# An adaLN block with a Mamba2 scan: the norm's application behind a decayed product, the gates' rows spread over three engines, the signs one step later

## The chip, the cores and the metric

The kernel runs on one core of a Trainium2 chip. The metric is the device time of one execution in microseconds (us), as the median of several runs. The core's engines work in parallel, each through its own instructions in a fixed order: TensorE (PE, matrix products and transposes, its weight loads shown as PEld), VectorE (DVE), ScalarE (ACT), GpSimd (POOL) and SyncE (SP), which here issues most of the DMA transfers.

## The reference

The input x has 4 sequences of 512 tokens with 512 features. A row `c` for each sequence gives six modulation vectors, two of which are gates.

```python
x = L0_attn_input_
mod = (_silu(L0_c) @ L0_wmod).reshape(L0_c.shape[0], 6, 1, -1)
sa, ca, ga, sb, cb, gb = (mod[:, 0], mod[:, 1], mod[:, 2], mod[:, 3], mod[:, 4], mod[:, 5])
ga = (2 * (ga >= 0) - 1) * jnp.maximum(jnp.abs(ga), 0.25)
gb = (2 * (gb >= 0) - 1) * jnp.maximum(jnp.abs(gb), 0.25)
h = _layernorm(x, axis=-1) * (1 + ca) + sa
x = x + ga * _L0_attn_ref(h, ...)
h = _layernorm(x, axis=-1) * (1 + cb) + sb
x = x + gb * _L0_ffn_ref(h, L0_ffn_weight, L0_ffn_bias)
```

`_L0_attn_ref` is a Mamba2 block. One projection gives x, B, C, z and the step dt. x, B and C go through a causal convolution over 4 tokens and a SiLU. A scan in chunks of 128 tokens follows with 64 heads of 16 features; B and C have 64 states in 8 groups. Within a chunk, token s contributes to token l with the weight C·B times exp(-(sum of dt between them)): this is the "decay". The result, times SiLU(z), is projected back to 512 features. `_L0_ffn_ref` is one 512x512 layer whose weights are replaced by their signs, times the mean magnitude of each row (alpha), plus a bias.

## The kernel before

**Tiling and steps.** A sequence is cut into two halves of 256 tokens, eight halves h in all; a half has two chunks c, and a chunk four pairs gp of head groups. A pair is a unit (h,c,gp): 64 units, one for each step of the loop at L845. In one step the kernel first emits what its list `steps` holds for that step, then the C·B products of two new units (`burst`, every other step), then `stage2` of the step's unit (its products with the decay, py) and last `stage0` and `stage1` of the unit two steps ahead, the "newest" one.

**The decays.** There are four decay tiles of 128x1024, two (r=0 and r=1) for a unit, so a tile is used by every second unit. `stage0` has SP load the sums into it by two DMAs (`load_sums`, L541 and L542, 256 and 128 KB); they can go when PE has read the tile for the last time. `stage1` makes the mask `gm`, has ACT take eight exps for each tile (L549) and DVE multiply by the mask (L625, "the decayed product"). `stage2` then has PE take py from it. Some decays of the last half are made ahead in the space of the projection's weights (`AHEAD`).

**The next half's front.** `FRONT` (L787) says at which step, counted from eight steps ahead of the half, each part is emitted: the load of x, then `f_norm` (the first layer norm) at step 2, `f_hT` at step 3 (PE's transposes phT, L330, and ACT's application of the modulation into hT, L347), `f_dt` (pa, L368), the projections pp_B, pp_C, pp_x (L434) with their convolutions on DVE (u_B, u_C, u_x, L454), and pp_z with uz (L516).

**The tails.** After a chunk's four units, `tail1` (L729) projects the result back (po), multiplies by the gate, adds the residual (xr) and takes the second layer norm into t. `tail2` comes a step later (PE's transposes ph at L757, ACT's h at L759), `tail3` two steps later (pf, L775; o at L777 and L778; the store res<-o by SP at L779).

**The layer norm.** `layer_norm` (L289) takes statistics on DVE, a power on POOL (rs, L298), and applies them on DVE at L300, at once. The tile t is single (`bufs=1`).

**The gates' rows.** `late_mods` (L233, once, in the second step) makes four of the modulation rows as one tile of 128x512, four lanes of which hold each vector, at lanes 0, 32, 64 and 96. Its last part (L250 to L262) makes the two gates and gate times bias on DVE and stores them by SP to `gate_d`; `load_gates` (L717) later spreads them over all lanes for a sequence, 768 KB. SP takes its DMAs in order: one that waits for its data holds up those behind it. Behind these stores stands, among others, the load of `wout` (L265).

**The signs.** `signs(o)` (L269) loads 128 rows of the ffn weights, sums their magnitudes on DVE (L274), takes the signs on DVE (L277) and scales them on ACT (L278). It runs for o=0 to 3 at steps 2 and 3, and `turned_signs` transposes them from step 5 on.

**Order.** A scheduling layer keeps the order of emission for each engine, apart from what is placed by `tc.issue_after(...)`: that makes the instructions inside it come after the one named, on their engines' lists. The fences `newest[...]` hold the last instruction of a kind for that use.

Of the kernel before, what the change touches and what calls it, by code (L numbers as in the profile page):

```python
# [11 lines left out]
F32 = mybir.dt.float32  # L12
AF = mybir.ActivationFunctionType
ALU = mybir.AluOpType
AX = mybir.AxisListType
# [3 lines left out]
B, L, DM = 4, 512, 512  # L19
# [8 lines left out]
NHALF = B * L // T  # L28
# [12 lines left out]
def adaln_mamba_block(  # L41
# [15 lines left out]
    nc = tc.nc  # L57
# [6 lines left out]
    def bc_mid(ap, n):  # L64

        return ap.unsqueeze(1).to_broadcast([ap.shape[0], n, ap.shape[1]])
# [4 lines left out]
    wk = ctx.enter_context(tc.tile_pool(name="wk", bufs=2))  # L71
# [47 lines left out]
    gate_d = dram.tile([B, 3, DM], F32, name="gate_d")  # L119
# [25 lines left out]
    def load_wm_at(t6, place, k0=0):  # L145

        n = place.shape[1]
        nc.sync.dma_start(place, wm_v[:, k0 : k0 + n, t6 * DM : (t6 + 1) * DM])
        for k in range(n):
            wms[t6, k0 + k] = place[:, k]  # L150
# [27 lines left out]
    room = wk.tile([P, 3, DM], F32, tag="gates", name="wm3_g", bufs=1)  # L178
    room_z = wm_tiles(3, "z", 6, 2)

    def load_late(h):

        load_wm_at(2, wout[:, 0:NK])
        load_wm_at(5, wout[:, NK:])
        load_wm_at(4, bwT)
        for k in range(2):
            load_wm_at(3, room_z[k].unsqueeze(1), k)
        load_wm_at(3, room[:, 0:2, :], 2)


    sc = keep.tile([P, NK, 32], F32, name="sc")
# [17 lines left out]
    def glued(products, after=None):  # L209

        with tc.issue_after(after) if after else nullcontext():
            first = products[0]()  # L212
        with tc.issue_after(first.ins), tc.high_priority(offset=1000):
            for product in products[1:]:
                product()  # L215
# [17 lines left out]
    def late_mods(h):  # L233

        pg = ps.tile([P, DM], F32, tag="mm", name="pg")
        glued([
            partial(
                mm, pg[32 * j : 32 * j + 32, :], sc[:, k, :], wms[t6, k], start=(k == 0), stop=(k == NK - 1)
            )
            for k in range(NK) for j, t6 in enumerate((2, 5, 4, 3))  # L240
        ])
        row = wk.tile([P, DM], F32, tag="t", name="rows", bufs=1)
        nc.vector.tensor_copy(row, pg)
        pm = ps.tile([P, NK, P], F32, tag="mm", name="pm")
        for dt in range(NK):
            nc.tensor.transpose(pm[:, dt, :], row[:, dt * P : (dt + 1) * P], ident)
        nc.vector.tensor_copy(modT[:, 2], pm[:, :, 96 : 96 + B])
        nc.vector.tensor_scalar(modT[:, 3], pm[:, :, 64 : 64 + B], 1.0, None, ALU.add)

        g = row[0:64, :]  # L250
        sg = wk.tile([64, DM], F32, tag="h2", name="sg")
        ab = wk.tile([64, DM], F32, tag="h2", name="ab")
        brow = wk.tile([64, DM], F32, tag="th", name="brow")
        second = slice(32, 32 + B)
        nc.sync.dma_start(brow[second, :], ffn_b.partition_broadcast(B))
        nc.vector.tensor_scalar(sg, g, 0.0, 2.0, ALU.is_ge, ALU.mult)
        nc.vector.scalar_tensor_tensor(ab, g, -1.0, g, ALU.mult, ALU.max)
        nc.vector.tensor_scalar(ab, ab, 0.25, None, ALU.max)
        nc.vector.scalar_tensor_tensor(sg, sg, -1.0, ab, ALU.add, ALU.mult)
        nc.vector.tensor_mul(ab[second, :], sg[second, :], brow[second, :])  # L260
        for i, v in enumerate((sg[0:B, :], sg[second, :], ab[second, :])):
            nc.sync.dma_start(gate_d[:, i, :], v)  # L262

    def load_wout():
        nc.sync.dma_start(wout, w_outT.rearrange("(k p) e -> p k e", p=P))  # L265
# [3 lines left out]
    def signs(o):  # L269

        fw = wk.tile([P, DM], F32, tag="h2", name=f"fw{o}")
        nc.sync.dma_start(fw, ffn_w[o * P : (o + 1) * P, :])
        alpha = wk.tile([P, 1], F32, tag="rs1", name=f"alpha{o}")
        nc.vector.tensor_reduce(alpha, fw, AX.X, ALU.add, apply_absolute_value=True)  # L274
        sw = wk.tile([P, DM], F32, tag="CB"[o % 2], name=f"sw{o}", bufs=3)

        nc.vector.tensor_scalar(sw, fw, 0.0, 0.5, ALU.is_ge, ALU.subtract)  # L277
        nc.scalar.activation(sw, sw, AF.Identity, scale=alpha)  # L278
        sws[o] = sw
# [9 lines left out]
    def layer_norm(tiles, name, into=None):  # L289
        n = len(tiles)  # L290
        st = wk.tile([P, n, 6], F32, tag=f"st{n}", name=f"st_{name}")
        mv = wk.tile([P, n, 2], F32, tag=f"mv{n}", name=f"mv_{name}")
        rs = wk.tile([P, n], F32, tag=f"rs{n}", name=f"rs_{name}")
        for j, t in enumerate(tiles):
            nc.vector.bn_stats(st[:, j, :], t)
            nc.vector.bn_aggr(mv[:, j, :], st[:, j, :])
        nc.vector.tensor_scalar(rs, mv[:, :, 1], EPS, None, ALU.add)
        nc.gpsimd.tensor_tensor(rs, rs, mhalf[:, :n], ALU.pow)  # L298
        for j, t in enumerate(tiles):
            nc.vector.tensor_scalar(  # L300
                into[j], t, mv[:, j, 0:1], rs[:, j : j + 1], ALU.subtract, ALU.mult
            )


    H = [dict(B={}, C={}, xt={}, xs={}, bt={}, z={}) for _ in range(NHALF)]
# [132 lines left out]
    newest = {}  # L438
# [105 lines left out]
    def exps(h, c, gp, ets):  # L544
        hd0 = c * NH + gp * HPP
        for r in range(2):
            for i in range(HPG):
                hd = hd0 + r * HPG + i
                nc.scalar.activation(  # L549
                    ets[r][:, i, :], ets[r][:, i, :], AF.Exp, bias=H[h]["st"][:, hd : hd + 1], scale=-1.0  # L550
                )
# [60 lines left out]
    def stage1(h, c, gp):  # L612

        n = f"{h}_{c}_{gp}"
        ets, e = U0.pop((h, c, gp))
        gm = wk.tile([P, 2, CH], F32, tag="gm", name=f"gm_{n}", bufs=3)  # L620
        nc.vector.tensor_mul(gm, G.pop(((h, c, gp), 0)), bc_mid(upto, 2))
        if (h, c, gp) not in AHEAD:
            exps(h, c, gp, ets)
        for r in range(2):
            nc.vector.scalar_tensor_tensor(  # L625
                ets[r], ets[r], 1.0, bc_mid(gm[:, r, :], HPG), ALU.min, ALU.mult
            )
        U1[h, c, gp] = (ets, e)

    def stage2(h, c, gp):  # L630
# [84 lines left out]
    gates = {}  # L715
# [13 lines left out]
    def tail1(h, c):  # L729
        b = h // HPB  # L730
        x2 = tails[h, c]
        po = ps.tile([P, DM], F32, tag="mm", name=f"po_{h}_{c}")
        last = (h, c) == (NHALF - 1, 1)
        for g in range(NKI):
            if last and g == NKI - 2:

                with tc.issue_after(last_po.ins):
                    tail2(h, 0)
            last_po = mm(po, H[h]["z"][g // 2][:, g % 2, c * CH : (c + 1) * CH], wout[:, g, :],  # L739
                         start=(g == 0), stop=(g == NKI - 1))  # L740
        t = wk.tile([P, DM], F32, tag="t", name=f"t_{h}_{c}", bufs=1)
        nc.vector.tensor_mul(t, po, gates[b][:, 0, :])
        nc.vector.tensor_add(x2, x2, t)
        layer_norm([x2], f"f{h}_{c}", [t])
        nc.gpsimd.tensor_add(x2, x2, gates[b][:, 2, :])
        tails[h, c] = (x2, t)
        if last:
            with tc.issue_after(last_po.ins):
                tail3(h, 0)
# [64 lines left out]
    def at(step, f, *args):  # L814
        steps.setdefault(step, []).append((f, args))

    for h in range(NHALF):
        for step, f, args in (FIRST, SECOND)[h] if h < 2 else FRONT:
            at(max(0, h - 1) * NU + step, f, h, *args)
        if h % HPB == 0:  # L820
            at(h * NU + 3, load_gates, h // HPB)
        if h == 0:
            at(0, load_late, h)
            at(1, behind, 0, late_mods)
            at(2, load_wout)
            for o in range(NK):
                at(o // 2 + 2, signs, o)
    for o in range(NK):
        at(o // 2 + 5, behind, 1, turned_signs, o)
    for h in range(NHALF):  # L830
# [9 lines left out]
    h = NHALF - 1  # L840
# [4 lines left out]
    for step in range(-1, max(steps) + 1):  # L845
        for f, args in steps.get(step, []):
            f(*args)

        new = units[step + 2 : step + 3] if step >= 0 else units[0:2]
        if step < 0:  # L850
            burst([], new)
            for unit in new:
                stage0(*unit)
                stage1(*unit)
        elif step < len(units):
            if step % 2 == 0 and (step + 2 < len(units) or not is_first(*units[step][:2])):
                burst(units[step : step + 2], units[step + 2 : step + 4])
            stage2(*units[step])
            for unit in POST.get(step, []):
                ahead(*unit)  # L860
            for unit in new:
                stage0(*unit)
                stage1(*unit)


_OUT = ((B, L, DM), np.float32)
# [39 lines left out]
```

## Time and profile before

| | |
|---|---|
| median of 3 runs | 736.62 us (733.73 to 736.94) |
| profiled execution | 737.38 us, of which the span from first to last instruction is 735.7 |
| mean granted TensorE clock | 0.993 |
| PE busy | 700.4 us (95%) |
| DVE, ACT, POOL busy | 599.5 (81%), 522.0 (71%), 254.8 us (35%) |
| HBM traffic | 92.47 MB read, 5.79 MB written |
| L549, decay exps on ACT | 960 instructions, 293.9 us |
| L625, decayed products on DVE | 120 instructions, 160.8 us |

The page gives busy times of the engines, and a chain of work that ended last, with its share by engine. The timeline gives for each instruction or run of like ones its start, its duration, engine, line, operation and tiles, and in brackets how long the engine was idle before it and what released it. Windows give the busy time of each engine in a stretch, with the granted clock of TensorE and the moved bytes.

### The profile page before, as it was taken

Reading aid. Unit: us, or ns where it says so; the run is one execution under the profiler, and the core shown is the slowest. Engines: PE = TensorE matmul, PEld = TensorE weight load, DVE = VectorE, ACT = ScalarE, POOL = GpSimd, SP = SyncE. Lnnn points to the kernel's source line nnn. Section 1 sums busy time; section 2 is a strip of 40 time slices with the busy share of each in tenths; the row PEclk is TensorE's granted clock in tenths of the full one; section 3 lists DMA queues with packets and bytes.
Section 4 is the critical chain, followed back from the end, with each engine's and each line's share of the span. In section 5 each row is a group of like instructions: output and inputs, shape, how many; then the busy total and the mean of one; then the engine's idle time right before and its main releaser. Section 6 shows DMA issues by size and latency. Waiting matters only on the chain.

```text
span 735.7 us, 15007 instructions
## 1 busy us (share of the span) xinstructions
PE 700.4 (95%) x5196; PEld 500.8 (68%) x5196; DVE 599.5 (81%) x1170; ACT 522.0 (71%) x1507; POOL 254.8 (35%) x297
## 2 busy tenths in 40 slices
PE   6999979899999999999999999999999999999997
PEld 3786746666677666677677666776667866677754
DVE  3869888876998678986899768996799867996995
ACT  2467658748696697785976787865968768788941
POOL 4021323444243332343223342433414332333652
PEclk9999989999999999999999999999999999999999
DMA  8991693535555256444644256552564537457720
GB/s 279 328 291 41 204 208 85 135 98 142 127 132 144 63 155 137 102 115 102 159 116 130 53 116 168 142 137 53 140 132 114 130 86 176 116 150 151 142 69 29
DMA packets 119067, 99.24 MB, mean 135 GB/s; under 512 B 73984, under 2 KB 97152, under 8 KB 118992
## 3 DMA queue, kind: packets, MB, share of 16 engines
q1 hardware_dynamic: 117808, 96.39, 52.3%
q0 software_dynamic: 896, 1.38, 0.7%
q8 instruction: 41, 0.67, 0.4%
q10 hardware_dynamic: 288, 0.52, 0.2%
q14 instruction: 34, 0.28, 0.1%
HBM read 92.47 MB, written 5.79 MB: 134 GB/s over the span
## 4 chain that ended last, share of the span: by engine, by line
PE 65%; ACT 16%; DVE 9%; DMA 4%; issue 4%; POOL 1%; SPq 1%; ACTq 0%; DVEq 0%; POOLq 0%
PE po L739 14%; PE pp_x L434 11%; PE pp_z L434 10%; ACT decay L549 9%; PE pp_C L434 7%; PE pp_B L434 5%; PE pf L775 3%; PE py L212 2%; PE py L215 2%; DVE decay L625 2%; ACT h L759 2%; DVE u_x L454 2%; DMA fw<-in_ffn_w 2%; ACT win L549 2%; PE gy L215 2%
## 5 line engine op out<-in xcount | busy, mean ns | idle before, releaser
L549 ACT ACTIVATE decay<-decay,st 128x128 f32<-128x128 f32 x960 | 293.9, 395 | 4.2 <-DMA decay<-sums_d 3.7
L625 DVE SCALAR_TENSOR_TENSOR decay<-decay,gm 128x1024 f32<-128x1024 f32 x120 | 160.8, 1341 | 50.3 <-ACT decay L549 47.2
L434 PE MATMUL pp_x<-hT,win 128*128 128x259 f32 x512 | 120.7, 390 | 7.3 <-DVE u_C L454 7.3
L434 PE MATMUL pp_z<-hT,win 128*128 128x256 f32 x512 | 118.1, 383 | 0.0
L434 PEld LDWEIGHTS pp_x<-hT,win 128*128 128x128 f32 x512 | 96.9, 193 | 25.2 <-ACT decay L549 7.7
L739 PE MATMUL po<-wout,z 128*128 128x512 f32 x256 | 113.8, 595 | 0.0
L434 PEld LDWEIGHTS pp_z<-hT,win 128*128 128x128 f32 x512 | 94.3, 189 | 16.3 <-issue 3.5
L675 POOL TENSOR_TENSOR z<-yt,z 128x256 f32<-128x256 f32 x62 | 62.9, 1015 | 76.1 <-DVE yt L674 57.8
L454 DVE SCALAR_TENSOR_TENSOR u_x<-pp_x,cw,u_x 128x256 f32<-128x256 f32 x192 | 83.6, 474 | 1.3 <-ACT u_x L450 0.7
L739 PEld LDWEIGHTS po<-wout,z 128*128 128x128 f32 x256 | 47.5, 190 | 53.1 <-issue 52.4
L672 POOL TENSOR_TENSOR yt<-yt,xs 128x256 f32<-128x256 f32 x46 | 41.4, 899 | 106.3 <-DVE yt L671 78.6
L507 POOL TENSOR_TENSOR xs<-u_x,rr 128x512 f32<-128x512 f32 x32 | 42.7, 1334 | 79.2 <-DVE u_x L459 61.3
L516 ACT ACTIVATE uz<-pp_z,zb 128x256 f32<-128x256 f32 x64 | 27.5, 470 | 59.0 <-PE pp_z L434 59.0
L215 PE MATMUL py<-decay,xpad 128*32 128x128 f32 x1680 | 66.3, 276 | 0.0
L434 PE MATMUL pp_B<-hT,win 128*128 128x259 f32 x256 | 63.5, 396 | 2.7 <-ACT decay L549 1.9
L434 PE MATMUL pp_C<-hT,win 128*128 128x259 f32 x256 | 59.6, 384 | 1.1 <-DVE u_x L454 1.1
L775 PE MATMUL pf<-bwT,h 128*128 128x512 f32 (+1 forms) x136 | 59.0, 578 | 1.4 <-ACT h L759 1.3
L434 PEld LDWEIGHTS pp_B<-hT,win 128*128 128x128 f32 x256 | 47.4, 193 | 14.5 <-ACT decay L549 3.1
L450 ACT ACTIVATE u_x<-pp_x,cb,cw 128x256 f32<-128x256 f32 x64 | 35.3, 560 | 30.5 <-PE pp_x L434 30.4
L434 PEld LDWEIGHTS pp_C<-hT,win 128*128 128x128 f32 x256 | 47.8, 189 | 9.4 <-PE pn L424 1.4
L679 POOL TENSOR_TENSOR xd<-xpad,st 128x256 f32<-128x256 f32 x48 | 34.1, 727 | 55.8 <-PE pst L215 28.3
L212 PE MATMUL py<-decay,xpad 128*32 128x128 f32 x240 | 47.4, 279 | 3.2 <-issue 2.2
(157 smaller groups left out, 1080.9 us busy)
## 6 DMA issues: line engine op xcount, KB each, us to landing
decay<-sums_d SPq DMA_DIRECT2D x120, 256.0 KB
decay<-sums_d SPq DMA_DIRECT2D x120, 128.0 KB
rr<-r_d SPq DMA_DIRECT2D x64, 128.0 KB
e<-e_d SPq DMA_DIRECT2D x96, 64.0 KB
win<-in_w_inT SPq DMA_DIRECT2D x4, 1024.0 KB
xr<-in_x SPq DMA_DIRECT2D x16, 256.0 KB
res<-o SPq DMA_DIRECT2D x15, 256.0 KB
x<-in_x SPq DMA_DIRECT2D x14, 256.0 KB
```

The costliest lines, as they stand in the source:

```text
L212: first = products[0]()
L215: product()
L434: last = mm(pm, win[:, k, col : col + P], H[h]["hT"][:, k, lo:], start=(k == 0), stop=(k == NK - 1))
L450: nc.scalar.activation(u[:, j, :], pm[:, KS - 1 :], AF.Identity, bias=cb[:, t : t + 1], scale=cw[:, t, KS - 1 : KS])
L454: nc.vector.scalar_tensor_tensor(u[:, j, :], pm[:, k : k + T], cw[:, t, k : k + 1], u[:, j, :], ALU.mult, ALU.add)
L507: nc.gpsimd.tensor_tensor(xs, xc, rr, ALU.mult)
L549: nc.scalar.activation(ets[r][:, i, :], ets[r][:, i, :], AF.Exp, bias=H[h]["st"][:, hd : hd + 1], scale=-1.0)
L625: nc.vector.scalar_tensor_tensor(ets[r], ets[r], 1.0, bc_mid(gm[:, r, :], HPG), ALU.min, ALU.mult)
L672: ew.tensor_add(t, t, xs)
L675: ew.tensor_mul(zg, t, zg)
L739: last_po = mm(po, H[h]["z"][g // 2][:, g % 2, c * CH : (c + 1) * CH], wout[:, g, :], start=(g == 0), stop=(g == NKI - 1))
L775: mm(pf, h2[:, k, :], bwT[:, k, cols], start=(k == 0), stop=(k == NK - 1))
```

## The change

Three edits.

1. `layer_norm` no longer applies its statistics at once. The application goes as a function into a list `normed`, and at the end of the step, after `stage1` of the newest unit, everything in the list is issued behind `newest["decay"]`, the r=0 decayed product of that unit. Excepted are the first half's first norm and the last half's two tails (`AT_ONCE`). The add of gate times bias to xr goes into the list too, when there is one.
2. The gates' rows are made at step 2 in a function of their own, `late_gates`: one operation on DVE, the magnitude on ACT, three operations on POOL, and the stores go by POOL's queue. Their tiles lie in `room`, the place of the gates' tile, not in the slots of h2 and th; the bias is loaded with the late weights.
3. `signs` come one step later, and the sum of magnitudes is taken by ACT as it writes the magnitudes (`accum_out`), not by DVE.

```diff
@@ load_late
         load_wm_at(3, room[:, 0:2, :], 2)
+        nc.sync.dma_start(brow[second, :], ffn_b.partition_broadcast(B))
@@ late_mods
-        g = row[0:64, :]
-        sg = wk.tile([64, DM], F32, tag="h2", name="sg")
-        ab = wk.tile([64, DM], F32, tag="h2", name="ab")
-        brow = wk.tile([64, DM], F32, tag="th", name="brow")
-        second = slice(32, 32 + B)
-        nc.sync.dma_start(brow[second, :], ffn_b.partition_broadcast(B))
-        nc.vector.tensor_scalar(sg, g, 0.0, 2.0, ALU.is_ge, ALU.mult)
-        nc.vector.scalar_tensor_tensor(ab, g, -1.0, g, ALU.mult, ALU.max)
-        nc.vector.tensor_scalar(ab, ab, 0.25, None, ALU.max)
-        nc.vector.scalar_tensor_tensor(sg, sg, -1.0, ab, ALU.add, ALU.mult)
-        nc.vector.tensor_mul(ab[second, :], sg[second, :], brow[second, :])
+        late_row.append(row)
+
+    late_row = []
+    second = slice(32, 32 + B)
+    brow = room[0:64, 2, :]
+
+    def late_gates(h):
+        g = late_row.pop()[0:64, :]
+        sg, ab = room[0:64, 0, :], room[0:64, 1, :]
+        nc.vector.tensor_scalar(sg, g, 0.0, 0.5, ALU.is_ge, ALU.subtract)
+        nc.scalar.activation(ab, g, AF.Abs)
+        nc.gpsimd.tensor_scalar(ab, ab, 0.25, 2.0, ALU.max, ALU.mult)
+        nc.gpsimd.tensor_tensor(sg, sg, ab, ALU.mult)
+        nc.gpsimd.tensor_tensor(ab[second, :], sg[second, :], brow[second, :], ALU.mult)
         for i, v in enumerate((sg[0:B, :], sg[second, :], ab[second, :])):
-            nc.sync.dma_start(gate_d[:, i, :], v)
+            nc.gpsimd.dma_start(gate_d[:, i, :], v)
@@ signs
-        nc.vector.tensor_reduce(alpha, fw, AX.X, ALU.add, apply_absolute_value=True)
         sw = wk.tile([P, DM], F32, tag="CB"[o % 2], name=f"sw{o}", bufs=3)
+        nc.scalar.activation(sw, fw, AF.Abs, accum_out=alpha)
@@ layer_norm
-        for j, t in enumerate(tiles):
-            nc.vector.tensor_scalar(
-                into[j], t, mv[:, j, 0:1], rs[:, j : j + 1], ALU.subtract, ALU.mult
-            )
+        def apply():
+            for j, t in enumerate(tiles):
+                nc.vector.tensor_scalar(
+                    into[j], t, mv[:, j, 0:1], rs[:, j : j + 1], ALU.subtract, ALU.mult
+                )
+        if name in AT_ONCE:
+            apply()
+        else:
+            normed.append(apply)
+
+    normed = []
+    AT_ONCE = ("a0", f"f{NHALF - 1}_0", f"f{NHALF - 1}_1")
@@ stage1
         for r in range(2):
-            nc.vector.scalar_tensor_tensor(
+            ins = nc.vector.scalar_tensor_tensor(
                 ets[r], ets[r], 1.0, bc_mid(gm[:, r, :], HPG), ALU.min, ALU.mult
             )
+            if r == 0:
+                newest["decay"] = ins.ins
@@ tail1
-        nc.gpsimd.tensor_add(x2, x2, gates[b][:, 2, :])
+        add = partial(nc.gpsimd.tensor_add, x2, x2, gates[b][:, 2, :])
+        if normed:
+            normed.append(add)
+        else:
+            add()
@@ the list of steps
             at(2, load_wout)
+            at(2, late_gates, h)
             for o in range(NK):
-                at(o // 2 + 2, signs, o)
+                at(o // 2 + 3, signs, o)
@@ the loop, at the end of a step
                 stage0(*unit)
                 stage1(*unit)
+            while normed:
+                with tc.issue_after(newest["decay"]):
+                    normed.pop(0)()
```

## The prediction

> **What bounds the kernel now.** I read the busy shares first, then the chain of work that ended last, then the stretch around the deferred operations in the timeline.
>
> ```profile
> PE 700.4 (95%) x5196; PEld 500.8 (68%) x5196; DVE 599.5 (81%) x1170; ACT 522.0 (71%) x1507; POOL 254.8 (35%) x297
> ...
> PE 65%; ACT 16%; DVE 9%; DMA 4%; issue 4%; POOL 1%; SPq 1%; ACTq 0%; DVEq 0%; POOLq 0%
> ```
>
> TensorE (PE) is busy for 700.4 of 735.7 us. Its 35.3 us of idle time are all that a better order can win; any work that PE must newly wait for adds in full. So the question for each moved instruction is not which engine it loads but whether PE stands behind it.
>
> The stretch that follows is one half's (h=2) from the timeline (columns: start, duration, engine, line, operation).
>
> ```profile
> 165.02 0.94 DVE L300 TENSOR_SCALAR t<-xr,mv_f,rs_f 128x512 f32<-128x512 f32 x1 [0.34 <-POOL rs_f L298]
> ...
> 167.41 0.60 PE L757 MATMUL ph<-ident,t 128*128 128x128 f32 x4
> 167.51 0.84 ACT L516 ACTIVATE uz<-pp_z,zb 128x256 f32<-128x256 f32 x2 [9.08 <-PE pp_z L434]
> ...
> 168.71 2.45 ACT L549 ACTIVATE decay<-decay,st 128x128 f32<-128x128 f32 x8
> ...
> 171.19 1.32 DVE L625 SCALAR_TENSOR_TENSOR decay<-decay,gm 128x1024 f32<-128x1024 f32 x1 [1.12 <-ACT decay L549]
> ...
> 178.79 0.49 SPq L541 DMA_DIRECT2D decay<-sums_d  x1
> 179.03 2.44 ACT L549 ACTIVATE decay<-decay,st 128x128 f32<-128x128 f32 x8
> 179.06 1.09 PE L330 MATMUL phT<-ident,x 128*128 128x128 f32 x8
> ...
> 180.81 0.68 DVE L778 TENSOR_TENSOR o<-o,xr 128x512 f32<-128x512 f32 x1
> ...
> 181.51 0.34 SPq L779 DMA_DIRECT2D res<-o  x1
> ```
>
> To be seen: t is normed at 165.02, and PE transposes it (ph) at 167.41 without a wait, while the decayed product of the newest unit (L625) comes only at 171.19, behind its eight exps. Today norm and product are independent; the norm wins the race by 6 us. The tile phT at 179.06 is likewise taken with no wait, its x normed steps earlier, though the decay tile that the new order puts in front of it has only just been requested (178.79).
>
> The norm's own waits, which the change can remove, are these (waiter, releaser, sum, count, longest):
>
> ```profile
> DVE t L300 <- POOL rs_f L298: 12.8, 16, 1.4
> ...
> DVE x L300 <- POOL rs_a L298: 3.4, 6, 0.8
> ```
>
> They are VectorE's (DVE's), 16.2 us in all. DVE is busy 81%, and the ph and phT above did not wait for it; a shorter queue there buys PE little.
>
> **The deferral, place by place.** All instances but a0 and the last half's two tails are put behind the r=0 product of the newest unit. The instruction order on each engine, as the changed program builds, tells what stands just ahead of the transposes.
>
> Tail of chunk 1 (six times, units (1..6,0,2)). PE now has pp_z2, pt_xt, py of the unit before, then ph2, and pst, pp_z3, pf behind it. DVE has the product, then t. The product needs exps that stand on ScalarE (ACT) behind uz and xpad, and uz needs pp_z2. Thus pp_z2's end (163.41+3.72=167.13) starts a round trip PE, ACT, DVE, PE: exps end 171.16, product 171.19+1.32, t 0.68 (the same line alone; 0.94 here), hence ph at about 173.2. PE without ph is through at 168.4. It loses 4.8 us (4.2 to 5.2).
>
> Norm of the next half (six times, h=2..7). New order on PE: py of unit 2 (both r), py of unit 3 (both r), phT, pa, pst, pp_B. On DVE: decay2, decay3, z, the two o, decay0, then x. On SyncE (SP): res<-o stands ahead of decay0's two loads. I replay h=2 with the rows above. From 173.2: ph 0.6, pst 0.5, pp_z3 3.7, pf 3.7 end at 181.7; gy 0.9 and py 1.0 let decay0's tile go at 183.2, and py of unit 3 (1.3) leaves PE empty at about 185. On DVE decay3's product follows the exps of 179.03 (end 181.47), so 182.7; z 0.68 and two o of 0.68 end at 184.7; res 0.34; loads at 185.1 and 185.6. How long a load takes from issue to use is seen elsewhere:
>
> ```profile
> 547.20 0.62 SPq L542 DMA_DIRECT2D decay<-sums_d  x1
> ...
> 552.25 2.45 ACT L549 ACTIVATE decay<-decay,st 128x128 f32<-128x128 f32 x8 [0.91 <-DMA decay<-sums_d]
> ```
>
> That is 5.05 us; the chain has one of 3.93. From 185.6: data at 189.5 to 190.7, exps +2.45, product +1.23, x +0.68: phT at 193.9 to 195.1. Here x cannot be early, because SP, ACT and DVE all have the decay in front of it. After phT come hT (1.9, on ACT behind decay1's exps too) and pa, so pp_B starts at 197.7 to 198.9. It started at 184.19: +13.5 to +14.7, the 4.8 included. If res did not hold the loads back, they would go at 183.2+0.6 and the same sum gives pp_B at 195.6, +11.4. I take 13.5, nearest to the row order as built: 6 x 13.5 = 81 us (68 to 88). Behind the waiting phT all of the half's projections are queued, and behind those everything else.
>
> Halves 3, 5, 7 have the gates' load (768 KB) on SP ahead of decay0 as well. The rows bound it by the moved rates: 322 GB/s in one window gives 2.4 us, 197 gives 3.9; none if it lands during the exps. I take 3 x 3 = +9 (0 to 12).
>
> Tail of chunk 0 (seven times): ph (before at 207.49) now follows six u_x and a product that ran at 208.91 and can start some 0.9 earlier; with t that is 209.6 to 210.9, PE being free at 208.5 to 208.8. +1.2 each, 8 in all (3 to 17). The add on xr that moves to behind (POOL, 1.3 us) has two steps until it is read; POOL is 35% busy, so it costs nothing, and 1.3 a time if that cover were gone.
>
> **The clock.** A long wait has a second price.
>
> ```profile
> 98.00:100.00 2.00, 0.59 (x2) 0.53 (x3) 2.00 (x7) 2.00 (x8) 0.00 (x0) 0.50 1.02 294
> 100.00:102.00 2.00, 2.00 (x6) 1.62 (x5) 2.00 (x6) 1.10 (x3) 0.00 (x0) 0.50 1.11 322
> 102.00:104.00 2.00, 2.00 (x6) 1.52 (x6) 2.00 (x5) 0.71 (x2) 0.45 (x1) 0.50 1.08 170
> ...
> 99.41 6.23 PE L434 MATMUL pp_x<-hT,win 128*128 128x259 f32 x16 [5.36 <-DVE u_C L454]
> ```
>
> After the one idle time of 5.36 us the granted clock (the column ahead of the last two) was 0.50, and 16 matmuls took 6.23 us, not 3.5 to 3.7: 2.6 us lost. The stall ahead of phT is 9 to 10 us, so I expect the same there, less what hides in the waits for hT: 2 each, +12 (0 to 16).
>
> [...]
>
> **The gates' rows and signs (once, h=1).** DVE loses 0.42+0.68+0.41+0.67+0.99 less 0.42 of gates and 4 x 0.69 of sums: about 5.5 us. ACT gains an Abs of 64x512 and four of 128x512; no such row exists, L278 on the same tile is 0.72, a plain pass of 256 columns 0.42: 2 to 4 us. POOL gains three passes (rows of 128x512: 1.33; at 64 partitions I take the same as the upper end, half as the lower) and three stores, 0.65 each by its own e_d row. SP takes brow's 8 KB early and loses three stores, two of them blocking: ab<-brow stood at 77.66 and held wout to 81.79, so fw landed at 95 and PE lost the 5.36 us. Wout can go near 73 and fw land near 88. Against it: the Abs waits for the rows (69.7) ahead of decay0's exps on ACT, and x_1 stands behind products and z, at about 81.3 rather than 74.37: pp_B near 85 rather than 80.46, a loss of some 5. By the replay PE reaches the late pp_x at 97.5 rather than 99.41, with a shorter stall: -3, with ends -8 (5.36+2.6 all gone) and +5.
>
> **Sum.** 81+9+8+12-3 = 107. PE's idle time in the steady halves is 35.3-6.2 (start)-4.65 (end)-5.4, about 19 us, 2.7 per half, 1.2 of it already in the replay; of the rest the new waits take in perhaps 4. So +103 on the profiled execution's 737.4 (span 735.7 and 1.7 outside; the median, 736.62, is 0.8 lower): 840.
>
> **Rivals.**
> - On the other side: the order does not bind; the exps and loads run far enough ahead that every product is done when its norm is ready. Then only the start shows: 5.36+2.6 = 8 gone, 729 us. For it: ACT has 29% free, and the changed order at the start does free SP early. Against: exps of the newest unit wait for a tile that PE is still reading at 178.7. It decides if decay0's product ends before 168 in the row of 171.19. Chance 0.08.
> - The low ends: loads go before res, the clock stays up, the start gains 8: 68+3-8 = 63, less 4: 796. For it: ACT and SP may drift ahead in long stalls. 0.27.
> - The high ends: clock lost at both stalls and res later: 88+12+8+16+8 = 132: 869. For it: 9 us of idle is far over 5.36. 0.15.
> - The deferral and the start cancel, or do nothing: 0.02.
>
> The forecast, 820 to 860, has 0.48. The range from 780 to 880 leaves out the first rival and the ends beyond. A difference under 0.5% (3.7 us) can't be told from none with this measurement: faster 0.08, same 0.02, slower 0.90.
>
> **What would show it.** Right: idle time ahead of ph L784 of 4 to 5 us, six times, and of 8 or more ahead of phT, six times, each put down to DVE; x right after a decay product; granted clock 0.50 after phT; PE's busy share near 84%; fw landing before 92. Wrong: phT starting within 2 us after py, or the decay's loads issued before res with the exps early, or PE's idle time under 60 us in all.

## The result, and the profile after

The changed kernel takes 848.73 us (median of 4 runs, 845.54 to 849.55) against 736.34 us before (4 runs): a ratio of 1.153 with a 95% interval of 1.149 to 1.157. The forecast was 840 us with a range of 780 to 880.

The page of the changed kernel, busy shares and the chain of work that ended last:

```profile
PE 726.2 (86%) x5196; PEld 522.4 (62%) x5196; DVE 594.0 (70%) x1162; ACT 527.4 (62%) x1516; POOL 262.3 (31%) x303
...
PE 58%; ACT 13%; DMA 11%; DVE 9%; issue 5%; SPq 3%; POOL 0%; ACTq 0%; DVEq 0%; POOLq 0%
```

The span went from 735.7 to 847.8 us, 112.1 more. PE has the same 5196 instructions, and two things happened to it: its idle time rose from 35.3 to 121.6 us (+86.3), and its busy time from 700.4 to 726.2 (+25.8), although it does the same work. The second part is a slower clock (mean 0.993 before, 0.929 after).

Who waits for whom after the change (waiter, releaser, sum, count, longest):

```profile
ACT decay L569 <- DMA decay<-sums_d: 66.7, 14, 11.6
...
PE phT L350 <- DVE x L311: 57.4, 8, 10.5
...
PE ph L784 <- DVE t L311: 41.9, 15, 6.6
...
DVE t L311 <- POOL rs_f L307: 1.1, 2, 0.7
```

The last line is the wait that the deferral takes away: DVE's wait for the power on POOL fell from 12.8 us to 1.1. In its place PE itself waits 99 us for DVE at the two transposes, and ACT waits 66.7 us for the decays' loads, where it had waited 3.7. The page before shows that in the row of the exps (count, busy us, mean ns, idle time ahead of them and what ended most of it):

```profile
L549 ACT ACTIVATE decay<-decay,st 128x128 f32<-128x128 f32 x960 | 293.9, 395 | 4.2 <-DMA decay<-sums_d 3.7
```

The same stretch of the timeline that the prediction showed (h=2), after the change:

```profile
173.40 1.22 DVE L645 SCALAR_TENSOR_TENSOR decay<-decay,gm 128x1024 f32<-128x1024 f32 x1 [1.81 <-ACT decay L569]
...
174.54 0.54 DVE L311 TENSOR_SCALAR t<-xr,mv_f,rs_f 128x512 f32<-128x512 f32 x1
...
175.23 1.09 PE L784 MATMUL ph<-ident,t 128*128 128x128 f32 x4 [4.16 <-DVE t L311]
...
177.30 5.64 PE L454 MATMUL pp_z<-hT,win 128*128 128x256 f32 x16
...
187.93 0.34 SPq L806 DMA_DIRECT2D res<-o  x1
...
188.38 1.90 SPq L561 DMA_DIRECT2D decay<-sums_d  x1
...
190.33 0.62 SPq L562 DMA_DIRECT2D decay<-sums_d  x1
...
194.24 4.78 ACT L569 ACTIVATE decay<-decay,st 128x128 f32<-128x128 f32 x16 [9.76 <-DMA decay<-sums_d]
...
196.71 1.23 DVE L645 SCALAR_TENSOR_TENSOR decay<-decay,gm 128x1024 f32<-128x1024 f32 x1 [5.01 <-ACT decay L569]
...
197.85 1.00 DVE L311 TENSOR_SCALAR x<-x,mv_a,rs_a 128x512 f32<-128x512 f32 x2
198.45 2.00 PE L350 MATMUL phT<-ident,x 128*128 128x128 f32 x8 [8.04 <-DVE x L311]
...
202.63 3.78 PE L454 MATMUL pp_B<-hT,win 128*128 128x259 f32 x16
```

Here each step of the wait can be read as one line: the tile is loaded, the exps wait for the load, the product for the exps, x for the product (it could have been applied long before), PE for x. The transposes take 2.00 us, where they took 1.09: in the window from 198 to 200 us the granted clock is 0.50. It is 0.50 from 176 to 180 us too, behind the wait at ph: pp_z takes 5.64 us there, where it took 3.72.

### The profile page after: what moved, and what is told of

It reads as the page before. It is cut to its first block, busy times and chain, and to the rows that moved or that the text cites. A ratio compares the mean times of both kernels' runs of the same rounds, so it can differ in the third digit from the quotient of the medians.

```text
span 847.8 us, 15019 instructions
## 1 busy us (share of the span) xinstructions
PE 726.2 (86%) x5196; PEld 522.4 (62%) x5196; DVE 594.0 (70%) x1162; ACT 527.4 (62%) x1516; POOL 262.3 (31%) x303
## 4 chain that ended last, share of the span: by engine, by line
PE 58%; ACT 13%; DMA 11%; DVE 9%; issue 5%; SPq 3%; POOL 0%; ACTq 0%; DVEq 0%; POOLq 0%
PE pp_z L454 12%; PE po L761 9%; DMA decay<-sums_d 9%; ACT decay L569 8%; PE pp_x L454 7%; PE pf L802 5%; PE pp_B L454 5%; PE pp_C L454 4%; DVE decay L645 2%; ACT win L569 2%; PE pa L388 2%; PE phT L350 2%; PE py L213 2%; PE py L216 2%; PE ph L784 1%
## 5 line engine op out<-in xcount | busy, mean ns | idle before, releaser
L569 ACT ACTIVATE decay<-decay,st 128x128 f32<-128x128 f32 x960 | 292.8, 393 | 67.0 <-DMA decay<-sums_d 66.7
L454 PE MATMUL pp_z<-hT,win 128*128 128x256 f32 x512 | 126.7, 403 | 0.0
L454 PE MATMUL pp_x<-hT,win 128*128 128x259 f32 x512 | 118.4, 385 | 0.6 <-DVE u_x L474 0.6
L454 PEld LDWEIGHTS pp_z<-hT,win 128*128 128x128 f32 x512 | 100.6, 202 | 19.5 <-issue 3.5
L474 DVE SCALAR_TENSOR_TENSOR u_x<-pp_x,cw,u_x 128x256 f32<-128x256 f32 x192 | 87.1, 478 | 4.6 <-ACT u_x L470 2.9
L697 POOL TENSOR_TENSOR z<-yt,z 128x256 f32<-128x256 f32 x62 | 51.7, 834 | 94.0 <-DVE yt L696 71.2
L701 POOL TENSOR_TENSOR xd<-xpad,st 128x256 f32<-128x256 f32 x48 | 37.3, 793 | 89.8 <-PE pst L216 51.2
L350 PE MATMUL phT<-ident,x 128*128 128x128 f32 x64 | 15.8, 425 | 57.4 <-DVE x L311 57.4
L216 PE MATMUL py<-decay,xpad 128*32 128x128 f32 x1680 | 64.6, 275 | 0.0
L527 POOL TENSOR_TENSOR xs<-u_x,rr 128x512 f32<-128x512 f32 x32 | 50.1, 1568 | 43.9 <-DVE u_x L479 30.5
L454 PEld LDWEIGHTS pp_B<-hT,win 128*128 128x128 f32 x256 | 49.9, 201 | 11.2 <-issue 2.5
```

The lines of the kernel that those rows point to most:

```text
L454: last = mm(pm, win[:, k, col : col + P], H[h]["hT"][:, k, lo:], start=(k == 0), stop=(k == NK - 1))
L474: nc.vector.scalar_tensor_tensor(u[:, j, :], pm[:, k : k + T], cw[:, t, k : k + 1], u[:, j, :], ALU.mult, ALU.add)
L527: nc.gpsimd.tensor_tensor(xs, xc, rr, ALU.mult)
L569: nc.scalar.activation(ets[r][:, i, :], ets[r][:, i, :], AF.Exp, bias=H[h]["st"][:, hd : hd + 1], scale=-1.0)
L697: ew.tensor_mul(zg, t, zg)
L701: nc.gpsimd.tensor_tensor(xd, xg, by_head(H[h]["ed"][:, hd0 : hd0 + HPP]), ALU.mult)
```

## The experiments

Each experiment changes the kernel before or the changed kernel in one respect. Times are medians; the ratios, with their 95% intervals, stand against runs of the kernel before on the same chip. Its medians lay between 735.55 and 736.56 us, so times of runs on different chips compare to about 1 us.

**The norm applied at once, the other two edits kept.**

```diff
-        if name in AT_ONCE:
+        if True:
             apply()
```

> Every norm is applied at once again; the other two edits stay. If the deferral is the whole loss, the time falls from 848.7 to that of before or a little under it, 731 to 736 us (the trace of the changed kernel has the start 2.3 us ahead at its second pair of pbw transposes). If the gates' rows or the later signs cost something that the deferral only covers, it stays above 740.

Measured: 738.12 us, ratio 1.0029 (1.0011 to 1.0047). That is 2 us above the first case: the deferral makes nearly all of the loss (110.6 of 112.4 us), and the other two edits together win nothing; they are slower by 0.1 to 0.5%. DVE no longer waits for the ffn weights at the start, though they are first used later than before (ACT at 99.78, not DVE at 95.13), and other waits of PE stand there:

```profile
102.14 3.60 PE L454 MATMUL pp_x<-hT,win 128*128 128x259 f32 x8 [3.69 <-DVE u_C L474]
...
124.07 0.66 PE L784 MATMUL ph<-ident,t 128*128 128x128 f32 x4 [2.86 <-DVE t L311]
```

These are two rows of PE's timeline of this run. Before, the first wait was 5.36 us and ended at 99.41; it is shorter now but ends later, and the second is new.

**The deferral alone, the other two edits undone.** The diff is that of the change without its hunks for the gates and signs.

> Only the norm's deferral, with gates' rows and signs as before. Theory: 840 to 848 us, since the start loses its 2.3 us again, but the 6.65 us wait of the first ph, which has the later signs' ACT operations ahead of its exps, shrinks to some 1.5 us. Rival, the edits add up with no interplay: 850 to 852.

Measured: 844.09 us, ratio 1.1455 (1.1424 to 1.1487), which is within the first range. So with the deferral in place the other two edits cost 4.6 us more. The first ph, which waits 6.65 us in the changed kernel, has no wait here (122.13).

**Only the next half's norms deferred.**

```diff
-        if name in AT_ONCE:
+        if name in AT_ONCE or name[0] == "f":
             apply()
```

> Only the next half's norms (a1 to a7) are deferred, both tails' norms are applied at once; the other edits stay. If the stalls add up, the time falls by the ph waits (41.9 us) and their slow clock (some 15): about 792 us. If the wait at phT is set by the decays' own chain (exps, products, o, res, loads) and swallows most of the 4.2 us that PE loses at ph before it, it falls only by the chunk-0 tails and a little: 815 to 830 us. That is my replay's reading.

Measured: 792.01 us, ratio 1.0752 (1.0728 to 1.0777). The time is that of the case in which the stalls add up; my replay's reading, that the wait at phT would swallow the one before it, fell. PE's rows of this run show why (h=2):

```profile
188.44 0.27 PE L213 MATMUL py<-decay,xpad 128*32 128x128 f32 x1 [1.71 <-ACT decay L569]
...
190.66 0.42 PE L213 MATMUL py<-decay,xpad 128*32 128x128 f32 x1 [1.57 <-DVE decay L645]
...
195.58 2.00 PE L350 MATMUL phT<-ident,x 128*128 128x128 f32 x8 [3.84 <-DVE x L311]
```

In this kernel the order on DVE and SP is another one too: o stands ahead of the older unit's last product, and the store of the result behind the first tile's loads. PE's wait at phT is 3.84 us, not 8.04, with two smaller waits at py ahead of it. A replay with the order of one kernel does not carry to another.

**Only the tails of chunk 1 deferred.**

```diff
-        if name in AT_ONCE:
+        if name in AT_ONCE or name[-2:] != "_1":
             apply()
```

> Only the norms of the tails of chunk 1 (f0_1 to f6_1) are deferred; the other edits stay. The 4.2 us wait at ph stands six times, with the clock lost after each: 733 + 6 x (4.2 + 1 to 2.5) = 764 to 773 us if nothing later takes it in. If the clock stays up with a 4.2 us wait alone: about 758. If PE's later waits take it in: under 750.

Measured: 782.26 us, ratio 1.062 (1.0593 to 1.0648), above every case that I had named. The six waits of 4.15 or 4.16 us stand as expected, and PE's busy time rose by 14.1 us against the run with all norms at once (714.6 and 700.5, at mean granted clocks of 0.967 and 0.993). Behind them a third cost stands that I had not counted: behind each of the six, PE has a further wait of 1.35 to 2.90 us for h, 11.0 us in all, such as

```profile
217.45 0.33 PE L439 MATMUL pn<-ident,sh 128*128 128x128 f32 x1 [1.38 <-ACT h L786]
...
309.46 3.45 PE L454 MATMUL pp_B<-hT,win 128*128 128x259 f32 x8 [2.90 <-ACT h L786]
```

In the second row the eight products took 3.45 us. Other rows of eight in this run have 1.99 to 2.02 (at 304.58, 491.91 and 679.58); the run with the deferral behind the product before has 1.99 at a granted clock of 1.00 (at 312.34). So part of the 14.1 us comes from these shorter waits.

**The same, with ph emitted behind the step's products, and with work in the wait.** The first of three kernels moves the emission of `tail2` of chunk 1 behind `stage2`. The others add products of the identity with `wout` to it, overwritten by the transposes that follow; nothing needs them. The diff shows only these products, of the second kernel.

```diff
+        if c == 1 and h < NHALF - 2:
+            with tc.issue_after(newest["py"]):
+                for i in range(8):
+                    mm(pt.rearrange("p k t -> p (k t)"), ident, wout[:, i % 8, :], start=True, stop=True)
         for dt in range(NK):
             nc.tensor.transpose(pt[:, dt, :], xn[:, dt * P : (dt + 1) * P], ident)
```

> As with the chunk-1 tails alone deferred, but ph and its tail2 are emitted behind stage2 of the same step, so that pst stands ahead of ph on PE. This is the ground for the next run. The wait ahead of ph shrinks by pst's 0.5 us, the rest stays: 775 to 785 us, PE's busy time some 14 us above that with all norms at once, as in the run with these tails alone.

Measured: 769.77 us, ratio 1.0466 (1.0448 to 1.0483). It is below the range, and 12 us faster than with the old place of ph, more than pst's 0.5 us each can explain; the waits ahead of ph are still 3.87 to 3.98 us, but PE's busy time is 8.2 us above that with all norms at once, not 14, and the further waits are shorter.

> The same, with eight extra 128x512 products (identity, results overwritten by the transposes) ahead of ph, six times: 3.4 us of work that nothing needs, just where PE waits. If the wait's second price is the granted clock, PE's busy time without the fillers (20 us) falls back to about 700 us, the clock to 0.99, and the time falls by 6 x 1.5 to 2.4 against the run without them, to 765 to 773 us. If the clock is not the wait's doing, or the fillers stand in the way, the time stays or rises by up to 6 x 1.

Measured: 782.87 us. The eight products took 7.13 us, where I had reckoned 3.4, an estimate that no row shows, in a wait of 4, so they stood in the way (6 x 3.2 = 19 us) and cost 13, more than the second case had named. The clock stayed up, though: its mean is 0.987, against 0.976 without them.

> Four extra products ahead of ph rather than eight: by the run with eight (7.13 us for eight) they take 3.6 us, a little less than the wait of 3.9 to 4.0 that they stand in. If the wait costs PE its clock, the clock stays at 1.00 there and pp_z behind it takes 3.6 us, not 5.0 to 5.6: 769.8 - 6 x 1.3 to 2 = 758 to 762 us. If the slow clock is not due to the wait: 769 to 772.

Here `range(8)` is `range(4)`. Measured: 757.48 us, ratio 1.0285 (1.0243 to 1.0328), 12.3 below the kernel without fillers. Windows of 2 us of the kernel without fillers, at the first of its six waits (columns: stretch and its length, busy us of PE, PEld, DVE, ACT and POOL with the number of instructions, then the granted clock, the DMA share and GB/s):

```profile
172.00:174.00 2.00, 0.24 (x2) 0.27 (x3) 2.00 (x3) 2.00 (x9) 1.64 (x2) 0.97 0.98 208
174.00:176.00 2.00, 2.00 (x8) 1.73 (x7) 1.83 (x2) 1.54 (x6) 1.34 (x1) 0.50 0.18 38
```

PE's timeline of the same kernel there:

```profile
173.76 1.01 PE L785 MATMUL ph<-ident,t 128*128 128x128 f32 x4 [3.98 <-DVE t L312]
174.56 4.96 PE L455 MATMUL pp_z<-hT,win 128*128 128x256 f32 x16
```

and PE's timeline of the one with four products, at the same place, and then a window of that kernel:

```profile
168.55 3.70 PE L787 MATMUL ph<-wout,ident 128*128 128x512 f32 x8
172.51 0.66 PE L789 MATMUL ph<-ident,t 128*128 128x128 f32 x4 [0.27 <-DVE t L312]
173.00 3.62 PE L455 MATMUL pp_z<-hT,win 128*128 128x256 f32 x16
```

```profile
174.00:176.00 2.00, 2.00 (x11) 1.76 (x10) 1.27 (x1) 2.00 (x8) 0.19 (x1) 1.00 0.00 1
```

Filled, the wait leaves pp_z at 3.62 us; unfilled, it took 4.96. PE's busy time without the fillers is 722.3 - 6 x 3.70 = 700.1 us, that of the kernel with all norms at once. So the slow clock is the wait's doing, at 3.98 us already (0.50 unfilled, 1.00 filled), and doing useless work there is faster than doing nothing. Not all of the 12.3 us is from there: in the profiled executions 3 us were ahead before the first filler ran (the first ph at 120.94 against 123.98).

**The result's stores on ACT's queue**, so that none stands ahead of the decays' loads.

```diff
-            nc.sync.dma_start(out[...], o)
+            nc.scalar.dma_start(out[...], o)
```

> The changed kernel, with the stores of the result on ACT's queue, so that none stands ahead of a decay's loads on SP. My prediction put some 2 to 3 us per half on that place (7.3 to 10.3 with and without): 848.7 - 6 x 2.5 = 834. The trace of the changed kernel speaks for less: the store goes at 187.93, and the tile is free for the loads only at about 188.2, so the time stays at 845 to 849.

Measured: 857.23 us, ratio 1.1633 (1.1611 to 1.1655), slower than the changed kernel and than both cases. The six waits at phT (h=2 to 7) sum to 52.8 us, against 51.3 with the stores on SP, so the store's place had not been their price. The rows of the changed kernel say the same for h=2: the store goes out at 187.93 and takes 0.34 us, and the load follows at 188.38, while PE reads the tile until about 188.0. PE's busy time is 5.1 us higher and its idle time another 5.1; what in the new order makes these I did not follow up.

**The deferral behind the product of the unit before.**

```diff
             stage2(*units[step])
+            while normed:
+                with tc.issue_after(newest["decay"]):
+                    normed.pop(0)()
             for unit in POST.get(step, []):
...
-            while normed:
-                with tc.issue_after(newest["decay"]):
-                    normed.pop(0)()
```

> The changed kernel, with the deferred norms issued before stage1 of the newest unit, so that they follow the r=0 product of the unit before it, which is done by then. The deferral as such stays. If the loss is the wait for the newest unit's exps and loads, the time falls to 736 to 745 us. If deferring the norms is itself the cost, it stays above 780.

Measured: 770.28 us, ratio 1.0449 (1.0409 to 1.049), between the two cases. 78 of the 112 us go when the norms no longer stand behind the newest unit's product. But the deferral behind an older one still costs 32 us over the kernel with all norms at once, which I had not expected; in the profiled executions 19.3 us of it are PE's busy time (719.8 against 700.5) and 14.3 its idle time. PE's rows and the clock there (h=2):

```profile
183.13 0.27 PE L213 MATMUL py<-decay,xpad 128*32 128x128 f32 x1 [1.86 <-ACT decay L569]
...
185.35 0.42 PE L213 MATMUL py<-decay,xpad 128*32 128x128 f32 x1 [1.57 <-DVE decay L645]
...
186.36 1.97 PE L350 MATMUL phT<-ident,x 128*128 128x128 f32 x8
```

```profile
182.00:184.00 2.00, 0.64 (x16) 0.41 (x16) 1.99 (x5) 1.60 (x6) 0.82 (x1) 1.00 0.55 166
184.00:186.00 2.00, 0.65 (x14) 0.60 (x16) 2.00 (x2) 0.00 (x0) 1.80 (x2) 0.64 0.76 239
186.00:188.00 2.00, 2.00 (x17) 1.54 (x8) 1.61 (x5) 0.27 (x1) 0.24 (x1) 0.50 0.75 197
```

In the kernel before, phT stood between the two units' py and gave PE something to do while the exps and the product of the later unit ran:

```profile
178.05 0.30 PE L212 MATMUL py<-decay,xpad 128*32 128x128 f32 x1
...
179.06 1.09 PE L330 MATMUL phT<-ident,x 128*128 128x128 f32 x8
...
180.99 0.27 PE L212 MATMUL py<-decay,xpad 128*32 128x128 f32 x1 [0.84 <-issue]
```

With x behind a product, phT comes after that py, and PE waits for both of its decays.

**Only the tails of chunk 0 deferred.**

```diff
-        if name in AT_ONCE:
+        if name in AT_ONCE or name[-2:] != "_0":
             apply()
```

> Only the norms of the tails of chunk 0 (f0_0 to f6_0) are deferred; the other edits stay. By the trace of the changed kernel the ph there waits 1.3 to 2.2 us five times and 6.65 at the first, of which 2.9 stand with all norms at once too: 738 + 4 + 10 + a slow clock of 0 to 4 = 750 to 756 us. With the other two parts (+53.9 and +44.1 us) that closes the whole of +110.6, if parts add up.

Measured: 737.84 us, ratio 1.0021 (1.0002 to 1.0039). The expected 750 to 756 fell: alone it costs nothing. Here ph waits 6.3 us for DVE in all, 2.87 of it at the first, as with all norms at once. Over that kernel (738.12) the three parts alone cost 53.9, 44.1 and -0.3, together 97.7 of the 110.6 us. The 12.9 us that are left come with the parts together; the waits at chunk 0's ph, which sum to 15.6 us in the changed kernel, are the likely place, though no run shows that they are all of it.

**Two single edits at the start, on the kernel before.** The first only swaps two lines of the list of steps, so that the ffn weights' first loads go ahead of `wout`; the second puts the gates' stores on POOL's queue and loads the bias early.

```diff
-            at(2, load_wout)
             for o in range(NK):
                 at(o // 2 + 2, signs, o)
+            at(2, load_wout)
```

> The kernel before with one thing changed: the two first loads of the ffn weights (256 KB each) are issued ahead of wout (2 MB), not behind it. They should land near 86 us, not 95, and the wait of 5.36 us at the second pp_x, with its slow clock of 2.6 us, should go: 728 to 733 us. Rival, the queue of DVE (u_B, u_C) is late for pp_x by itself: 734 to 737, no difference.

Measured: 733.38 us, ratio 0.9971 (0.996 to 0.9983): the only version faster than the kernel before, by 0.2 to 0.4%, and so than both; it lies between the two cases. The timeline shows the weights in use at 86 us rather than 95, and the late pp_x without the slow clock (1.00 from 96 to 102 us):

```profile
86.26 0.67 DVE L274 TENSOR_REDUCE alpha<-fw 128x1 f32<-128x512 f32 x1
...
96.50 3.74 PE L434 MATMUL pp_x<-hT,win 128*128 128x259 f32 x16 [1.81 <-DVE u_C L454]
```

```diff
-            nc.sync.dma_start(gate_d[:, i, :], v)
+            nc.gpsimd.dma_start(gate_d[:, i, :], v)
```

> The kernel before with the gates' three stores on POOL's queue and the bias loaded early; the rows stay on DVE, and norms, signs and sums as before. SP is then free of the two waits at 72.66 and 77.66 us; wout goes out near 72, and the ffn weights land before 90: 728 to 733 us if the late weights cost the 8 us there. If the gain is eaten by the order of DVE and ACT as with all norms at once: 735 to 739.

Measured: 739.93 us, ratio 1.0061 (1.0047 to 1.0074), slower, and above both cases. The weights do come earlier (alpha at 88.16), but the order of ACT and SP shifts with the edit, and PE's wait moves to another releaser:

```profile
98.27 2.71 PE L434 MATMUL pp_x<-hT,win 128*128 128x259 f32 x8 [4.04 <-ACT decay L549]
```

## Why the prediction was right, and where its steps were off

- **PE bounds, and new waits add in full.** Right: 86.3 us of idle time and 25.8 of slow clock make the 112.1. Forecast were about 91 of idle time and 12 of clock: the sum came near partly by luck, since too little clock was offset by some idle time too much. The relief of DVE (599.5 to 593.3 us busy with all norms at once) bought nothing.
- **Tail of chunk 1.** 4.8 us each were forecast, 4.16 came, six times; t itself took 0.54 rather than 0.68. But with these tails alone deferred the cost was 44.1 us. In the profiled executions it is 40.7, of which 26.6 are idle time and 14.1 busy time. The clock, and the 11.0 us of waits for h further on, are what the step "It loses 4.8 us" had left out; since 25.0 us of waits at ph and these 11.0 are more than 26.6, other waits shrank.
- **Norm of the next half.** The replay had PE wait 9 to 10 us; the six waits measure 7.00 to 10.49, 51.3 in all. pp_B of half 2 came at 202.63, 18.4 later than before. PE had run empty ahead of ph at 171.07 rather than 168.4, so 15.8 of it lie in this stretch, where 13.5 and 2 for the clock were forecast. The sum held. One of its terms did not: that res holds the loads back (13.5 against 11.4, some 2 us) was not what made the wait, as the run with the stores on ACT shows. The loads went as late as 188.38 since PE itself was late with its last reading of the tile: it had left ph 2 us later than replayed, and pp_z behind it took 5.64 us rather than 3.7 at the slow clock, which the replay had not charged there. The first load took 1.90 us to issue, not 0.49, and the exps began 3.91 us after the second was issued. That the total came out near is in part luck.
- **Gates' load in halves 3, 5 and 7.** Forecast 3 us each; the waits at phT there are 9.69 us on average against 7.41 in halves 2, 4 and 6, so 2.3.
- **Tail of chunk 0.** 8 us were forecast. The changed kernel has 15.6 us of waits there, 6.65 at the first, where the signs' operations, moved a step later, stand on ACT (from 117.36 on) ahead of most of the exps (from 120.74). Deferred alone, these norms cost nothing: the six ph behind the first wait 3.0 us in all, not 1.2 each.
- **The clock.** This term was mis-sized: 12 forecast, 25.8 measured. I charged only the stalls at phT, not the waits at ph. In the trace of before the longest wait of PE below 5.36 us is 1.93 us (at 132.44), with the clock at 1.00 behind it, so it shows nothing for the lengths between. The windows with and without fillers do: 0.50 behind a wait of 3.98 us unfilled, 1.00 filled. Shorter waits that were followed by 0.50 as well are named at the end.
- **The start.** -3 forecast; the second pair of pbw transposes is 2.3 us ahead (116.70 rather than 118.97), and the first ph's wait gives it back. `wout` went out at 68.51 rather than 81.79, earlier even than the 73 expected, but with the signs a step later the ffn weights are first used at 91.57, not 88, and phT of half 1 waits 5.81 us for x.
- **The rivals.** The one on the other side fell: its condition was a product ended before 168 us, and it ran at 173.40. Clock lost at both stalls, as the rival of the high ends has it, came true, and is why 848.7 lies above 840; the 16 in that rival's sum, an estimate for clock lost at the six ph (6 x 2.6, the loss behind 5.36 us), is a term that no run shows: with the tails of chunk 1 alone deferred the busy time rose by 14.1 us, the shorter waits for h among their causes, and by 8.2 with ph emitted later. What the last 8 of that sum stands for is not said. Of the signs named for being right, two of the six waits at phT fell short of 8 us (7.00 and 7.19).

## What to carry to other kernels

An instruction deferred behind another takes over everything that this one waits for, its loads, its engine's queue, its operand's last reader; before moving it, follow that chain back and ask who waits at the other end, on the engine that bounds the kernel. What was moved may also have fed the filler work of the bounding engine: here phT kept PE busy while a decay was made. Waits of some 4 us on PE, with the shorter ones behind them, cost 1.4 to 2.4 us each again in slow clock here (8.2 and 14.1 us for six), which belongs into the sum.

## What was not expected of the hardware

Two short waits of PE, 1.86 and 1.57 us with 0.65 us of work between them, were followed by a granted clock of 0.50 (from 186 to 188 us of the run with the deferral behind the product before), as the single wait of 3.98 us without fillers was (from 174 to 176 us). A single wait of 2.86 to 2.88 us at the first ph was followed by either: the four transposes took 0.66 us in the kernel with all norms at once (1.00 from 124 to 126 us), and 1.12 in the one behind the product before (0.50 from 124 to 128 us). In the changed kernel even waits of 2.19 and 2.02 us at ph (334.41 and 750.08) were followed by 0.50, in the windows from 336 to 338 and from 752 to 754 us, while behind one of 1.59 us (541.87) the clock stayed at 1.00. The trace does not show what else decides between the two. Four 128x512 products run as eight instructions and took 3.70 us, so 0.93 each.
